# Attention over 4 images: x transposed by VectorE in 32x32 blocks, and the ends of a group regrouped

## The chip, the cores and the metric

The kernel runs on one core of a Trainium2 chip. The metric is the device time of one launch in microseconds; the median of three runs stands for a kernel. A profile of one execution comes with it, taken by the hardware profiler: for each engine (PE is TensorE, PEld its weight loads, DVE is VectorE, ACT is ScalarE, POOL is GpSimd, SP is SyncE, which here only issues transfers) it lists every instruction with start and duration, what it waited for, and every DMA issue. DMA issued from SP and from POOL goes through two queues that share the core's 16 DMA engines.

## The reference

For each of 4 images with 4096 positions and 256 channels, self-attention and a residual:

```python
q = jnp.einsum('bwhc,cd->bwhd', x, Wq) + bq      # 128 wide
k = jnp.einsum('bwhc,cd->bwhd', x, Wk) + bk      # 128 wide
v = jnp.einsum('bwhc,cd->bwhd', x, Wv) + bv      # 256 wide
pq, pk, pv = q.reshape(B, -1, N), k.reshape(B, -1, N), v.reshape(B, -1, N)
energy = jnp.einsum('bcn,bcm->bnm', pq, pk)      # 4096 x 4096 per image
attention = softmax(energy, axis=-1)
out = jnp.einsum('bcm,bnm->bcn', pv, attention).reshape(B, W, H, C)
return gamma * out + x
```

The reshape is a plain one, without a transpose, so a row of pq is not a channel of one position: 32 consecutive positions of q fill one row of 4096. Everything is float32.

## The kernel before, in words

**Numbers in three parts.** To keep float32 accuracy with fast matmuls, every operand is split into three fp32r parts: h (a slightly shrunk copy, made by ScalarE), d and l (two corrections, made by VectorE from h and the original). Each product is then three fast matmuls. `split` (L153), `x_forms`, `qk_forms` and `v_pair_forms` make these parts.

**Steps.** Image b has 8 groups g of 512 query columns (`NG`), and each group 16 steps t (`NU`), each over 256 keys. The loop at L693 runs over all n = 0..511 steps; t is n modulo 16. One step on TensorE is 18 matmuls of 512 columns, in this order: `cross(n+2)` (2, then ScalarE scales them in PSUM), the first half of `attend(n, 0)` (6), `energy(n+2)` (4, then ScalarE takes the exponential into a tile x), pieces of the projection work, and `attend(n, 1)` (6). `upper` makes h of the exponentials on ScalarE, `halves(n+1)` makes l and d on VectorE (L418, L420) and adds the tile into the running softmax sum s (L403): three operations over 128x1024 per step. Buffers l and d have two copies, k three.

**Projections ride along.** While image b is attended, the q, k and v of image b+1 are computed in 16 steps per pair of x units (8 pairs per image). `step(p, engine)` (L555) puts the pieces into TensorE's, ScalarE's and VectorE's order by a count r; for most of the kernel r is t - 1 (modulo 16). At r = 0 (t = 1) TensorE transposes both units of x with a matmul against the identity (`transposed`, L214: 4 transposes of 128x128 per unit) into a PSUM bank; at r = 1..4 ScalarE and VectorE split it; at r = 5 and 6 come the q and k products, at r = 9 to 12 the v products. At r = 12 (t = 13) `load_x` (L200) asks SP to load the next pair of x into the buffer with tag xd. That buffer also holds the d parts of the present pair, so the load waits for the v products at t = 12. Image 0's x is done ahead of the loop, in its own way.

**End of a group.** At t = 15 `emptied(n, 0)` lets ScalarE copy two of the four PSUM accumulators into the tile o (tag o, a single buffer); at t = 0 VectorE empties the other two. Then `finish` (L464) runs as a generator that `proceed` advances once at the end of each step: SP stores both halves of the sum s to DRAM (zd) and reads them back regrouped as y (32 partitions by 4 rows, 8 transfers), so that VectorE can add over partitions: a reduction (L482), a 32x32 block transpose (L488), another reduction, a reciprocal. At t = 3 VectorE adds the two halves of o (L479), at t = 9 it multiplies by the reciprocal (L497), at t = 10 a POOL transfer adds x from DRAM into o (L501), and at t = 13 SP stores o to the output (L504).

**What sets the order.** Each engine's order is the order in which the program names its instructions. SP and POOL issue their transfers in this order too, and each waits at the head of its queue. A new tile with a tag waits until the readers and writers of the buffer's last tile are done, a DMA among them counting as done when it has landed. On SP, step t = 13 names first the x loads (they stand in the "act" part of `step`), later the store of o (`proceed`); the vf stores follow at t = 14 and 0, zd at t = 15, y at t = 0.

Of the kernel before, what the change touches and what calls it, by code (L numbers as in the profile page):

```python
# [9 lines left out]
F32 = mybir.dt.float32  # L10
# [3 lines left out]
ALU = mybir.AluOpType  # L14
AX = mybir.AxisListType
# [5 lines left out]
def kernel(  # L21
# [36 lines left out]
    nc = tc.nc  # L58
# [42 lines left out]
    with ExitStack() as fast:  # L101
# [13 lines left out]

        vall = qkv.tile([P, NU, 2, 3, C], F32R, tag="v", name="v")
        wf = qkv.tile([P, 2, 3, KC, C], F32R, tag="wf", name="wf")
        zd = dram.tile([B * NG, 2, P, NB], F32, tag="zd", name="zd", bufs=1)
        rd = dram.tile([B * NG, NB], F32, tag="rd", name="rd", bufs=1)
        xs4 = work.tile([P, 4, 2, XB], F32, tag="o", name="xs", bufs=1)  # L120
        raw = ppool.tile([P, 2, KC, C], F32, tag="x", name="raw")
# [66 lines left out]
        def bank(name, shape, b, ring):  # L188
            if b:
                tile_ = spare(name, shape)  # L190
                now["turn"] += 1
                return tile_
            pool, tag = next(rings[ring])
            return pool.tile(shape, F32, tag=tag, name=name)
# [5 lines left out]
        def load_x(b, i):  # L200
            if b == B or i >= NI:
                return
            if b == 0:
                t = xs4[:, i % 4]
                if i:
                    nc.sync.dma_start(t, xv[b, i])
                loads["x", b, i] = t
                return
            pair = work.tile([P, 2, 2, XB], F32, tag="xd", name=f"x_{b}_{i}", bufs=1)
            for u in range(2):  # L210
                nc.sync.dma_start(pair[:, u], xv[b, i + u])
                loads["x", b, i + u] = pair[:, u]

        def transposed(b, i):  # L214
            xs = loads.pop(("x", b, i))
            tp = units["xt", b, i] = bank(f"xt_{b}_{i}", [P, KC, 2, P], b, 0)
            for k in range(KC):
                for s in range(2):
                    nc.tensor.transpose(tp[:, k, s, :], xs[:, s, k * P : (k + 1) * P], ident)  # L219

        def x_forms(b, i):

            y = units.pop(("xt", b, i))
            if b == 0:
                if i % 3 < 2:
                    f = ppool.tile([P, 3, KC, 2, P], F32R, tag="ld", name=f"xf_{b}_{i}")
                else:
                    f = work.tile([P, 4, KC, 2, P], F32R, tag="xf", name=f"xf_{b}_{i}", bufs=1)
                f = [f[:, j] for j in range(3)]
            else:  # L230
                if i % 2 == 0:
                    shape = [P, 2, KC, 2, 2, P]
                    f = work.tile(shape, F32R, tag="xf", name=f"xf_{b}_{i}", bufs=1)
                    d = work.tile([P, *shape[2:]], F32R, tag="xd", name=f"xd_{b}_{i}", bufs=1)
                    now["xf"] = [f[:, 0], f[:, 1], d]
                f = [y_[:, :, i % 2] for y_ in now["xf"]]
            units["xf", b, i] = f
            yield from split(*f, y, b == 0 and i > 1)
# [156 lines left out]
        def halves(n):  # L395
            if n >= B * STEPS:
                return
            x, h = units[n]

            def summed():  # L400
                if n % NU:
                    s = now["s"]
                    nc.vector.tensor_tensor(s, s, x, ALU.add)  # L403
                else:
                    now["s"] = x

            def whole():
                s = now["sum"] = now["s"]
                nc.vector.tensor_tensor(s[:, 0, :], s[:, 0, :], s[:, 1, :], ALU.add)

            after = 0 < n < 5
            if not after:
                summed()
            if n == B * STEPS - 1:
                whole()
            ld = ppool.tile([P, 2, 2, NB], F32R, tag="ld", name=f"ld_{n}")
            l, d = ld[:, 0], ld[:, 1]
            nc.vector.tensor_tensor(l, x, h.bitcast(F32), ALU.subtract)  # L418

            nc.vector.scalar_tensor_tensor(  # L420
                d, h.bitcast(F32), 1.0 + E, x, ALU.mult, ALU.subtract
            )
            if n == 2:
                next(vs)
                next(vs, None)
            if after:
                summed()
            units[n] = h, l, d
# [35 lines left out]
        def finish(n, o, s):  # L464
            b, g = divmod(n, NG)
            r4 = rall[:, n, :]
            for i in range(2):
                nc.sync.dma_start(zd[n, i], s[:, i, :])
            yield
            y = q_tile(n, f"y_{n}", F32).rearrange("p j f a -> p (j f) a")  # L470
            for j in range(NJ):
                for i in range(2):
                    nc.sync.dma_start(
                        y[j * 32 : (j + 1) * 32, NJ * i : NJ * (i + 1)],
                        zd[n, i].rearrange("(a p) (j c) -> j p a c", p=32, j=NJ)[j],
                    )
            for _ in range(3):
                yield
            nc.vector.tensor_tensor(o[:, 0], o[:, 0], o[:, 1], ALU.add)  # L479
            for _ in range(3):  # L480
                yield
            nc.vector.tensor_reduce(  # L482
                y[:, 8].rearrange("p (f c) -> p c f", f=NJ),
                y[:, :8].rearrange("p a (c f) -> p c f a", f=NJ),
                AX.X,
                ALU.add,
            )
            nc.vector.transpose(y[:, 9], y[:, 8])  # L488
            nc.vector.tensor_reduce(r4, y[:, 9].rearrange("p (f c) -> p f c", f=NJ), AX.X, ALU.add)
            nc.vector.reciprocal(r4, r4)  # L490
            nc.sync.dma_start(rd[n, :].rearrange("(p j) -> p j", j=NJ), r4)
            yield
            r = o[:, 1, 0]
            nc.sync.dma_start(r, rd[n, :].partition_broadcast(P))
            yield
            yield
            nc.vector.tensor_tensor(  # L497
                o[:, 0], o[:, 0], r.unsqueeze(1).to_broadcast([P, 2, NB]), ALU.mult
            )
            yield  # L500
            nc.gpsimd.dma_start(o[:, 0], xg[b, g], accum_op=ALU.add)  # L501
            for _ in range(3):
                yield
            nc.sync.dma_start(og[b, g], o[:, 0])  # L504
# [50 lines left out]
        def step(n, engine):  # L555

            if n < 0:
                return
            b, u = divmod(n, STEPS)
            i, r = divmod(u, R)  # L560
            b, i = b + 1, 2 * i
            if b >= B:
                return
            made = now["made"]

            def begin(key, pieces):
                made[key] = pieces
                next(pieces)

            if engine == "pe":  # L570
                if r == 0:
                    transposed(b, i)
                    transposed(b, i + 1)
                elif r == 5:
                    products(b, i, 0, (2,))
                    products(b, i + 1, 0, (2,))
                elif r == 6:
                    products(b, i, 0, (0, 1))
                    products(b, i + 1, 0, (0, 1))
                elif r in (9, 11):  # L580
                    products_v(b, i, r // 11, (2,))
                elif r in (10, 12):
                    products_v(b, i, r // 12, (0, 1))
            elif engine == "act":
                if r in (1, 2):
                    begin(("x", r - 1), x_forms(b, i + r - 1))
                elif r in (7, 8):
                    begin(("qk", r - 7), qk_forms(b, i + r - 7))
                elif r in (10, 12):
                    seed_v_pair(b, i, r // 12)  # L590
                    if r == 12:
                        load_x(b + (i + 2) // NI, (i + 2) % NI)
                elif r in (11, 13):
                    begin(("v", r // 13), v_pair_forms(b, i, r // 13))
            else:
                if 1 <= r <= 4:
                    next(made["x", (r - 1) // 2])
                elif r == 5:
                    seed_qk(b, i)
                    seed_qk(b, i + 1)  # L600
                elif 7 <= r <= 10:
                    next(made["qk", (r - 7) // 2])
                    if r % 2 == 0:
                        next(made["qk", (r - 7) // 2], None)
                elif 11 <= r <= 14:
                    next(made["v", (r - 11) // 2])
                    if r % 2 == 0:
                        next(made["v", (r - 11) // 2], None)
# [355 lines left out]
```

## Time and profile before

| | |
|---|---|
| median of 3 runs | 2321.32 us (2320.11 to 2322.51) |
| the profiled execution | 2319.64 us |
| its span, first to last instruction | 2317.9 us |
| TensorE's granted clock | 0.999 |
| DMA | 445.30 MB, mean 192 GB/s |
| SP's queue / POOL's queue, share of 16 DMA engines | 20.6% / 45.5% |

The times in a profile row count from the first instruction of the span. A busy time is the union of the instructions' durations. Matmuls overlap in the pipeline, so the busy share of TensorE alone doesn't say that it was the limit; the chain of waits does: it is followed back from the last instruction, at each step to what released it. In a row of a group, the number after the bar is the busy time in us, then the mean of one in ns, then the idle time ahead of them. DVE operations overlap by some 0.08 us, so the time that one costs on its queue is the distance of two starts. For a transfer the duration is that of issuing it; the landing is told apart.

### The profile page before, as it was taken

To read this page: it belongs to the slowest core of one execution; us is meant where nothing else is said; L and a number is where in the kernel's file an instruction comes from. 1 tells how busy PE (TensorE), PEld (TensorE's weight loads), DVE (VectorE), ACT (ScalarE), POOL (GpSimd) and SP (SyncE) were. 2 spreads that over 40 slices of the span, in tenths; PEclk is the share of its full clock that TensorE was granted. 3 is DMA by queue.
4 is the path that set the end of the run, shared out by engine and by line. 5 is a ranking of instruction groups with operands and counts; after the bars stand their busy time and mean duration, and the time that the engine had idled before them with its cause. 6 is when DMAs were issued, how large, how long until landed. Compare 5 with 4: busy or idle time off the path is not lost.

```text
span 2317.9 us, 31970 instructions
## 1 busy us (share of the span) xinstructions
PE 2307.0 (100%) x10758; PEld 1931.5 (83%) x10758; DVE 2174.3 (94%) x2174; ACT 1796.9 (78%) x2917; POOL 417.1 (18%) x716
## 2 busy tenths in 40 slices
PE   9999999999999999999999999999999999999998
PEld 9888888888888888888888888888888888888887
DVE  8999999999999999999999999999999999888988
ACT  7778777787777777777777777777787777888775
POOL 7111111111221111111122111111112211111110
PEclk9999999999999999999999999999999999999999
DMA  8557765577896776666799667755679855455553
GB/s 273 162 168 207 206 176 154 170 204 205 266 268 184 208 207 179 166 170 194 201 292 267 186 182 207 199 167 165 173 223 289 258 140 141 141 136 149 154 150 97
DMA packets 232190, 445.30 MB, mean 192 GB/s; under 512 B 27986, under 2 KB 109652, under 8 KB 232020
## 3 DMA queue, kind: packets, MB, share of 16 engines
q0 software_dynamic: 101120, 280.54, 45.5%
q1 hardware_dynamic: 130352, 162.38, 20.6%
q8 instruction: 88, 1.44, 0.3%
q14 instruction: 82, 0.67, 0.1%
q10 hardware_dynamic: 548, 0.26, 0.0%
HBM read 321.92 MB, written 120.39 MB: 191 GB/s over the span
## 4 chain that ended last, share of the span: by engine, by line
PE 99%; DVE 0%; ACT 0%; DMA 0%; issue 0%; ACTq 0%; DVEq 0%
PE a L442 40%; PE e L383 20%; PE b L442 20%; PE e L368 10%; PE qv L257 5%; PE v L274 3%; PE xt L219 1%; DMA raw<-in_L_conv_Wk_dram 0%; ACT qv L292 0%; DVE xf L165 0%; PE zp L517 0%; DVE o_last L547 0%; DVE o_last L542 0%; DVE qv L285 0%; DVE o_last L548 0%
## 5 line engine op out<-in xcount | busy, mean ns | idle before, releaser
L386 ACT ACTIVATE x<-e 128x512 f32<-128x512 f32 x960 | 522.4, 596 | 323.6 <-PE e L383 323.5
L369 ACT ACTIVATE e<-e 128x512 f32<-128x512 f32 x1024 | 546.7, 571 | 132.2 <-PE e L368 132.2
L442 PE MATMUL a<-h,v 128*128 128x512 f32 x2048 | 633.5, 390 | 0.0
L442 PE MATMUL a<-ld,v 128*128 128x512 f32 x2048 | 630.9, 389 | 0.0
L442 PE MATMUL b<-ld,v 128*128 128x512 f32 x2048 | 630.8, 389 | 0.0
L418 DVE TENSOR_TENSOR ld<-x,h 128x1024 fp32r<-128x1024 f32 x480 | 584.6, 1218 | 35.1 <-ACT h L392 22.3
L403 DVE TENSOR_TENSOR s<-s,x 128x1024 f32<-128x1024 f32 x480 | 584.2, 1217 | 33.9 <-ACT x L386 32.6
L355 POOL DMA_DIRECT2D k<-kf x512 | 272.5, 532 | 1845.7 <-PE e L383 1745.2
L420 DVE SCALAR_TENSOR_TENSOR ld<-h,x 128x1024 fp32r<-128x1024 f32 x480 | 584.0, 1217 | 0.0
L383 PE MATMUL e<-q,k 128*128 128x512 f32 x2048 | 547.7, 389 | 0.0
L392 ACT ACTIVATE h<-x 128x1024 fp32r<-128x1024 f32 x480 | 510.5, 1064 | 14.3
L442 PEld LDWEIGHTS a<-ld,v 128*128 128x128 f32 x2048 | 384.4, 188 | 80.6
L442 PEld LDWEIGHTS b<-ld,v 128*128 128x128 f32 x2048 | 384.3, 188 | 80.3 <-DVE ld L420 0.2
L383 PEld LDWEIGHTS e<-q,k 128*128 128x128 f32 x2048 | 384.2, 188 | 79.7
L442 PEld LDWEIGHTS a<-h,v 128*128 128x128 f32 x2048 | 379.6, 188 | 74.2
L368 PE MATMUL e<-q,k 128*128 128x512 f32 x1024 | 315.5, 389 | 0.0
L368 PEld LDWEIGHTS e<-q,k 128*128 128x128 f32 x1024 | 191.9, 188 | 39.8
L310 DVE SCALAR_TENSOR_TENSOR f<-f,qv 128x512 fp32r<-128x512 f32 x128 | 85.5, 678 | 0.3
L418 DVE TENSOR_TENSOR ld<-s,h 128x1024 fp32r<-128x1024 f32 x32 | 39.2, 1226 | 46.8 <-ACT h L392 46.8
L257 PE MATMUL qv<-wf,xf 128*128 128x256 f32 x576 | 77.2, 285 | 0.9 <-DVE qv L285 0.4
L257 PEld LDWEIGHTS qv<-wf,xf 128*128 128x128 f32 x576 | 73.7, 191 | 4.1 <-DVE xf L165 0.8
L165 DVE SCALAR_TENSOR_TENSOR vf<-vf,v 128x512 fp32r<-128x512 f32 x96 | 65.2, 679 | 0.0
(88 smaller groups left out, 1126.8 us busy)
## 6 DMA issues: line engine op xcount, KB each, us to landing
k<-kf POOLq DMA_DIRECT2D x512, 384.0 KB, 3.6
vf<-vf SPq DMA_DIRECT2D x96, 384.0 KB, 5.1
v<-vf POOLq DMA_DIRECT2D x96, 384.0 KB, 6.3
kf<-f SPq DMA_DIRECT2D x128, 192.0 KB, 3.7
qd<-f SPq DMA_DIRECT2D x124, 192.0 KB, 3.8
q<-qd POOLq DMA_DIRECT2D x31, 768.0 KB, 6.0
zd<-s SPq DMA_DIRECT2D x62, 256.0 KB, 5.0
y<-zd SPq DMA_DIRECT2D x248, 64.0 KB, 4.4
```

The lines of the kernel that those rows point to most:

```text
L257: nc.tensor.matmul(to[:, s, :], left, right.rearrange("p s a -> p (s a)") if w else right, start=(f == 2 and s == k == 0), stop=(f == 1 an ...
L310: nc.vector.scalar_tensor_tensor(f[:, :, :, j, :], h.bitcast(F32), s, y, ALU.mult, op)
L355: nc.gpsimd.dma_start(t, kf[b, u % NU])
L368: nc.tensor.matmul(e, *forms(n, i, 2), start=True, stop=False, skip_group_check=True)
L369: nc.scalar.mul(e, e, -REST)
L383: nc.tensor.matmul(e, *forms(n, i, f), start=False, stop=(f == 1), skip_group_check=True)
L386: nc.scalar.activation(x[:, i, :], e, AF.Exp, scale=(1.0 + E) ** 3 / E)
L392: nc.scalar.activation(h, units[n], AF.Identity, scale=UPPER)
L403: nc.vector.tensor_tensor(s, s, x, ALU.add)
L418: nc.vector.tensor_tensor(l, x, h.bitcast(F32), ALU.subtract)
L420: nc.vector.scalar_tensor_tensor(d, h.bitcast(F32), 1.0 + E, x, ALU.mult, ALU.subtract)
L442: nc.tensor.matmul(to, vall[:, t, i, f, j * P : (j + 1) * P], units[n][f][:, i, :], start=(t == 0 and i == 0 and f != 1), stop=(t == NU - ...
```

## The change

Three things are changed.

1. For images 1 to 3, `transposed` is no longer 4 TensorE transposes per unit but one VectorE instruction over 128x512, which transposes within blocks of 32x32. To make the result the same, x has to lie differently in SBUF: row j of block q holds what belongs to channels 32q to 32q+31. So a unit is loaded by 8 transfers instead of 1, each of 32 partitions, in contiguous pieces of 32 floats. VectorE transposes at r = 1 and 2; the split's pieces move to r = 3 and 4, on VectorE two in each.
2. The two halves of o are added by a POOL transfer from o to o with accumulation, in place of VectorE's L479.
3. The halves of the sum s are added by VectorE (`whole`, 128x512) at the last step of every group, before the sum is stored; before, only the last group of all did this. So only one half is stored (1 transfer for 2), read back (4 for 8) and reduced (512 columns for 1024).

```diff
-        zd = dram.tile([B * NG, 2, P, NB], F32, tag="zd", name="zd", bufs=1)
+        zd = dram.tile([B * NG, P, NB], F32, tag="zd", name="zd", bufs=1)
...
             for u in range(2):
-                nc.sync.dma_start(pair[:, u], xv[b, i + u])
-                loads["x", b, i + u] = pair[:, u]
+                raw_x = pair[:, u].rearrange("p s f -> p (s f)")
+                for q in range(4):
+                    for k in range(KC):
+                        nc.sync.dma_start(
+                            raw_x[q * 32 : (q + 1) * 32, k * XB : (k + 1) * XB].rearrange(
+                                "j (s c i) -> j s c i", s=2, c=4
+                            ),
+                            xv[b, i + u].rearrange(
+                                "(c j) s (k q i) -> q k j s c i", j=32, k=KC, q=4
+                            )[q, k],
+                        )
+                loads["x", b, i + u] = raw_x
...
             tp = units["xt", b, i] = bank(f"xt_{b}_{i}", [P, KC, 2, P], b, 0)
+            if b:
+                nc.vector.transpose(tp.rearrange("p k s a -> p (k s a)"), xs)
+                return
...
-            if n == B * STEPS - 1:
+            if n % NU == NU - 1:
                 whole()
...
-            for i in range(2):
-                nc.sync.dma_start(zd[n, i], s[:, i, :])
+            nc.sync.dma_start(zd[n], s[:, 0, :])
             yield
             y = q_tile(n, f"y_{n}", F32).rearrange("p j f a -> p (j f) a")
             for j in range(NJ):
-                for i in range(2):
-                    nc.sync.dma_start(
-                        y[j * 32 : (j + 1) * 32, NJ * i : NJ * (i + 1)],
-                        zd[n, i].rearrange("(a p) (j c) -> j p a c", p=32, j=NJ)[j],
-                    )
+                nc.sync.dma_start(
+                    y[j * 32 : (j + 1) * 32, :NJ],
+                    zd[n].rearrange("(a p) (j c) -> j p a c", p=32, j=NJ)[j],
+                )
             for _ in range(3):
                 yield
-            nc.vector.tensor_tensor(o[:, 0], o[:, 0], o[:, 1], ALU.add)
+            nc.gpsimd.dma_start(o[:, 0], o[:, 1], accum_op=ALU.add)
             for _ in range(3):
                 yield
             nc.vector.tensor_reduce(
-                y[:, 8].rearrange("p (f c) -> p c f", f=NJ),
-                y[:, :8].rearrange("p a (c f) -> p c f a", f=NJ),
+                y[:, 4].rearrange("p (f c) -> p c f", f=NJ),
+                y[:, :NJ].rearrange("p a (c f) -> p c f a", f=NJ),
                 AX.X,
                 ALU.add,
             )
...
             if engine == "pe":
-                if r == 0:
-                    transposed(b, i)
-                    transposed(b, i + 1)
-                elif r == 5:
+                if r == 5:
...
             elif engine == "act":
-                if r in (1, 2):
-                    begin(("x", r - 1), x_forms(b, i + r - 1))
+                if r in (3, 4):
+                    begin(("x", r - 3), x_forms(b, i + r - 3))
...
             else:
-                if 1 <= r <= 4:
-                    next(made["x", (r - 1) // 2])
+                if r in (1, 2):
+                    transposed(b, i + r - 1)
+                elif r in (3, 4):
+                    next(made["x", r - 3])
+                    next(made["x", r - 3])
```

More of the change, by code (lines that the diff above doesn't have):

```diff
@@ L487, in finish @@
             )
-            nc.vector.transpose(y[:, 9], y[:, 8])
-            nc.vector.tensor_reduce(r4, y[:, 9].rearrange("p (f c) -> p f c", f=NJ), AX.X, ALU.add)
+            nc.vector.transpose(y[:, 5], y[:, 4])
+            nc.vector.tensor_reduce(r4, y[:, 5].rearrange("p (f c) -> p f c", f=NJ), AX.X, ALU.add)
             nc.vector.reciprocal(r4, r4)
```

## The prediction

> **What bounds the kernel now.** I read the busy times first, then the chain of waits, then one period of 16 steps by windows and by time, and last the DMA queue of SP. In the first fence: the page's busy times and its chain by engine; one period as a window (columns: length, then busy time and count of PE, weight loads, DVE, ACT, POOL, then clock, DMA share, GB/s); and pieces of the chain in order of time (start, length).
>
> ```profile
> PE 2307.0 (100%) x10758; PEld 1931.5 (83%) x10758; DVE 2174.3 (94%) x2174; ACT 1796.9 (78%) x2917; POOL 417.1 (18%) x716
> PE 99%; DVE 0%; ACT 0%; DMA 0%; issue 0%; ACTq 0%; DVEq 0%
> ...
> 815.85:887.66 71.81, 71.81 (x334) 60.00 (x334) 68.69 (x70) 55.77 (x91) 10.15 (x18) 1.00 0.65 183
> ...
> 860.40 0.91 PE e L383 x4
> 861.31 0.87 PE xt L219 x8
> 862.18 0.92 PE a L442 x4
> ...
> 887.66 1.91 PE qv L257 x16
> ```
>
> The chain is TensorE for 99%, and one period shows no gap in it: whatever leaves TensorE's stream is gained, and whatever makes TensorE wait is lost. VectorE has 71.81 - 68.69 = 3.1 us to spare per period. I write t for the step's number modulo 16; in the period shown, t = 0 begins with the `cross` matmuls at 854.34 (quoted below).
>
> **TensorE: the transposes go.** The eight transposes of a pair of x units take 0.87 us of the chain. Images 1 to 3 have 24 pairs (192 transposes in groups of 8), so 24 x 0.87 = 20.9 us are removed. Nothing is put on TensorE instead.
>
> **VectorE.** The rows by shape (count | busy us, mean ns | idle before), and the same engine in order of time, with the matmuls that need its results:
>
> ```profile
> L165 DVE SCALAR_TENSOR_TENSOR xd<-xf,xt 128x512 fp32r<-128x512 f32 x48 | 32.5, 677 | 0.0
> L482 DVE TENSOR_REDUCE y<-y 128x128 f32<-128x1024 f32 x31 | 61.7, 1991 | 0.0
> L488 DVE STREAM_TRANSPOSE y<-y 128x128 f32<-128x128 f32 x31 | 9.7, 312 | 1.1
> L409 DVE TENSOR_TENSOR s<-s 128x512 f32<-128x512 f32 x1 | 0.7, 691 | 0.0
> ...
> 846.45 1.23 DVE L418 TENSOR_TENSOR ld<-x,h 128x1024 fp32r<-128x1024 f32 x1 [0.45 <-PE b L442]
> 850.86 1.23 DVE L418 TENSOR_TENSOR ld<-s,h 128x1024 fp32r<-128x1024 f32 x1 [1.45 <-ACT h L392]
> 870.99 1.22 DVE L479 TENSOR_TENSOR o<-o 128x1024 f32<-128x1024 f32 x1
> 872.13 1.22 DVE L403 TENSOR_TENSOR s<-s,x 128x1024 f32<-128x1024 f32 x1
> 878.40 1.22 DVE L420 SCALAR_TENSOR_TENSOR ld<-h,x 128x1024 fp32r<-128x1024 f32 x1
> 879.54 0.68 DVE L165 SCALAR_TENSOR_TENSOR xf<-xf,xt 128x512 fp32r<-128x512 f32 x1
> 880.14 1.22 DVE L403 TENSOR_TENSOR s<-s,x 128x1024 f32<-128x1024 f32 x1
> 889.76 1.22 DVE L420 SCALAR_TENSOR_TENSOR ld<-h,x 128x1024 fp32r<-128x1024 f32 x1
> ...
> 881.08 0.61 PE L442 MATMUL b<-ld,v 128*128 128x512 f32 x2
> 892.16 0.61 PE L442 MATMUL b<-ld,v 128*128 128x512 f32 x2
> ```
>
> - Added: two 128x512 block transposes, at t = 2 and 3, where the L165 pieces of x stood. No row has this shape. The 128x128 one took 312 ns, so a 512-wide one lies between 0.31 us and four times that, 1.25. I take 0.68, what a 128x512 operation that touches PSUM took, and 0.60 of queue time (879.54 to 880.14): 1.2 us a period.
> - Gone: L479, 872.13 - 870.99 = 1.14 us. L482 reads half as much; between nothing and half of 1.99 us, I take 0.9.
> - Added: `whole` at t = 14, 0.69 us by L409, between two operations one of which sat idle 0.45 us and the next 1.45 us before it. I cost it at nothing; if those idles were gone it would be 0.6 a period.
>
> The sum is 1.2 - 1.14 - 0.9 + 0.6 = -0.2 us of VectorE a period, against 0.87 less TensorE time to hide in. The order matters more: the x pieces, one each at t = 2 to 5, become transposes at t = 2 and 3 and two pieces each at t = 4 and 5. At t = 5 operand d ended at 878.40 + 1.22 = 879.62 and its matmul began at 881.08, 1.46 us of slack; it gains 1.14, loses one piece (0.60) and the 0.87, and keeps 1.13. At t = 7 it is 892.16 - 890.98 = 1.18, plus 1.14 and 0.9, minus two pieces and 0.87: 1.15. So VectorE stays just behind TensorE, and I count no stall. With transposes of 1.25 us the 1.14 more would use all of this up.
>
> ScalarE's two x pieces move to t = 4 and 5, where they come between the `cross` scaling and the exponentials as they did before; nothing. The add of o's halves becomes one POOL transfer of 512 KB at t = 3. What is behind it on POOL is the next k load, which waits for TensorE anyway; what reads its result is L497 six steps later. Nothing, unless POOL's queue is full, which its 10.15 us of 71.81 does not show. The sum's transfers fall from 2 + 8 to 1 + 4 on SP: they are not waited for, nothing either way.
>
> **SP's queue: the part that can undo it.** At t = 13 two x loads become 16, and in SP's order the store of o (L504) stands behind them. The next `emptied` writes o (one buffer) at t = 15, so it waits for that store to land. Rows of this place (a q after the engine: its DMA queue), then the durations of the loads, the landing of the store in the last image, where no x load stands ahead, and of one store beside the v loads:
>
> ```profile
> 840.03 1.20 SPq L211 DMA_DIRECT2D x<-in_x_dram  x2
> 841.33 0.59 SPq L504 DMA_DIRECT2D out_dram<-o  x1
> 854.85 5.08 SPq L473 DMA_DIRECT2D y<-zd  x8
> ...
> 849.36 0.53 POOL L355 DMA_DIRECT2D k<-kf  x1 [4.46 <-PE e L383]
> ...
> 853.70 0.69 ACT L462 ACTIVATE o<-a,gam 128x512 f32<-128x512 f32 x1
> ...
> 854.34 0.62 PE L368 MATMUL e<-q,k 128*128 128x512 f32 x2
> 854.80 0.61 PE L442 MATMUL a<-h,v 128*128 128x512 f32 x2
> ...
> L211 SPq DMA_DIRECT2D x<-in_x_dram x48: 545/583/867, 68.1 to 1702.4; - x48
> ...
> L504 SPq DMA_DIRECT2D out_dram<-o x8: 543/544/545, 1841.1 to 2296.0; - x8
> ...
> DMA to landing us min/median/max: 3.0/3.0/7.2
> ...
> DMA to landing us min/median/max: 9.6/9.6/9.6
> ...
> k<-kf POOLq DMA_DIRECT2D x512, 384.0 KB, 3.6
> rd<-rall SPq DMA_DIRECT2D x31, 2.0 KB, 1.4
> ...
> q1 hardware_dynamic: 130352, 162.38, 20.6%
> ```
>
> The first x load goes out at 840.03, when the buffer xd comes free; call that the gate. ScalarE begins to empty a at gate + 13.67 and ends at 854.39; TensorE needs it at 854.80, 0.41 later. So the store may land up to gate + 14.08 for free, and TensorE waits for what is beyond. Behind `emptied` on ScalarE stand the scaling of e and the next h, on which VectorE's l and d of the next step wait; they are late by the same time, beside and not on top of it. Behind the x loads on SP stand, after the store, the vf and zd stores, some 9 us later than now: their buffers are written again some ten steps on, and the sum is read at t = 6, so nothing.
>
> When is it issued? Each new load moves 32 KB in 256 pieces of 128 B, as many pieces as an old one had of 1 KB (256 KB). Pace per load: at least 0.545 us; at most 1.27, if it went by pieces as in the y loads (5.08/8 = 0.635 for 128 pieces, one wait among them). I take 0.655: the second of the pair's 1.20 us is 0.61, and the gap to the next 0.04. Sixteen make 10.5 us, against 1.30 before. When does it land? 3.0 us after the issue undisturbed, 9.6 at worst. The k load issued at 849.36 (landing after 3.6) flies at the same time; I take 3.8. The store then lands at gate + 14.3, 0.2 us too late.
>
> 22 stores stand behind x loads: 24 pairs issue 23 loads (the last has nothing more to load), and the first of these comes before any store. Twenty at 0.2 make 4 us. Two lie beside the v loads, where the store took 9.6; between 3.8 and that I take 6.5, so gate + 17.0, 2.9 late: 6 us together. **Sum:** -20.9 + 4 + 6 = -11 us. The profiled execution took 2319.64 us (span 2317.9), 1.7 under the median of 2321.32; -11 on the median is **2310 us**. One tenth of a microsecond more per load is 1.6 us of lateness and 22 x 1.6 = 35 us: the forecast stands on an edge.
>
> **The rivals.**
> 1. *The store costs nothing* (pace 0.6 or less, landing 3.5 or less: gate + 13.1): 2321.3 - 20.9 = 2300 us. For it: the shortest load row, 0.545. Against it: that row is a load with none ahead.
> 2. *The wait eats the gain exactly:* stalls of 0.75 to 1.15 us in each period, within 0.2% of before (about what a measurement of this kernel tells from no change): 2317 to 2326.
> 3. *The other side: the store is late for good.* Place: ScalarE's `emptied` at t = 15. It decides from a pace of about 0.72 us per load (16 x 0.72 + 3.8 - 14.08 = 1.24 late, 22 x 1.24 = 27 us against 20.9). At 0.8 it is 2.5 late: 2321 - 21 + 55 + 6 = 2361; at 1.27, 10 late, 2520. For it: the y row's price per piece. Against it: the x rows.
> 4. *The small pieces themselves are slow.* The hardware queue's packets took 0.206 x 16 x 2317.9/130352 = 59 ns each at 1.25 KB. If 128 B cost as much, 16 x 256 of them over 16 engines take 15.0 us, the store lands at about gate + 15.0 + 3.0 = 18, 4 late: 2321 - 21 + 22 x 4 = 2388. Against it: rd's 2 KB, 128 pieces of 16 B, landed after 1.4 us. The Trainium skill, in "DMA: Bandwidth & Descriptors", section Specifications, speaks for this rival: it puts the smallest transfer for full rate at 512 B and says that a smaller one is read, changed and written. By that rule the time would be this rival's; the 1.4 us row shows no such price, though for a single small transfer.
> 5. *VectorE becomes the bound* (transposes over 1.25 us): another 0.5 us a pair is 24 x 0.5 = 12 us, so 2322 with my stalls. Against it: the 312 ns row.
>
> **How the numbers follow.** My forecast's case (stalls of 0 to 0.5 us, 2302 to 2317) 0.33; rival 1 0.12; rival 2 0.14; rival 3 0.29; rival 4 0.07; rival 5 0.05, mostly slower. Faster 0.45, same 0.14, slower 0.41. The range takes in all but the tails of rivals 3 and 4: 2299 to 2385; the likeliest case alone is 2302 to 2317.
>
> **What would show it.** After: no xt rows on TensorE beyond the 64 of image 0; a period near 70.94 us plus the stall; SP with 16 x rows of about 0.6 us, the store issued 10.5 us behind the first; ScalarE's L462 waiting for the DMA out_dram<-o, and TensorE idle before a at t = 0. The 128x512 transposes near 0.68 us. Pace over 0.7 or a store landing after more than 4.3 us makes me wrong upwards; a store landing within 3.5 us makes me wrong downwards; waits of TensorE for DVE ld (L420) would show that I mis-sized VectorE.

## The result, and the profile after

The changed kernel takes **2337.84 us** (median of 6 runs, 2332.99 to 2339.47) against 2321.27 before: a ratio of 1.0068, 95% interval 1.0056 to 1.0081. It is slower by 0.7%, inside the range and on the wrong side of the forecast.

The page of the changed kernel: busy times, and the chain by engine. Then its list of waits (in total us, times, longest us):

```profile
PE 2301.2 (99%) x10566; PEld 1916.1 (82%) x10566; DVE 2162.4 (93%) x2222; ACT 1798.1 (77%) x2917; POOL 446.5 (19%) x747
PE 84%; SPq 9%; DMA 5%; ACT 1%; issue 1%; DVE 0%; ACTq 0%; DVEq 0%
...
L228 DVE STREAM_TRANSPOSE xt<-x x48: 711/718/723, 82.6 to 1750.3; 128x512 f32<-128x512 f32 x48
```

```profile
ACT o L475 <- DMA out_dram<-o: 32.2, 22, 5.8
PE a L455 <- ACT o L475: 23.1, 20, 5.4
```

Before, the chain was 99% TensorE. Now SP's queue holds 9% of it, transfers 5%. VectorE got no busier. The waits name the place: ScalarE's emptying of the accumulators (L475 here, L462 before) waits 22 times for the store of o, and TensorE 20 times for ScalarE.

POOL loads the v of the next image around the end of an image (here 583 to 702 us and 1163 to 1282); a period with neither these loads beside it nor a stretch of halved clock is called quiet. One quiet period, and the worst one, as windows from one t = 0 to the next (columns as in the prediction); below them, the four stretches in which the granted clock was 0.5:

```profile
932.77:1004.36 71.59, 71.23 (x325) 59.11 (x325) 68.34 (x73) 55.78 (x91) 11.09 (x19) 1.00 0.67 184
566.90:643.54 76.64, 71.24 (x324) 59.12 (x324) 68.33 (x73) 55.78 (x91) 19.62 (x35) 0.98 0.89 258
...
641.20:648.00 6.80, 4.46 (x11) 3.49 (x12) 4.50 (x5) 3.81 (x6) 0.00 (x0) 0.50 0.93 351
1221.50:1228.30 6.80, 4.54 (x11) 3.61 (x12) 4.58 (x5) 3.80 (x6) 0.00 (x0) 0.50 1.03 390
1300.00:1303.40 3.40, 3.40 (x10) 2.62 (x9) 2.72 (x3) 2.52 (x5) 0.11 (x1) 0.50 1.04 411
1375.10:1378.50 3.40, 3.40 (x9) 2.67 (x8) 2.72 (x3) 2.41 (x5) 0.00 (x0) 0.51 0.69 260
```

Through the end of that quiet period, in two fences: the chain (start, length), then the timeline's rows of SP, ScalarE and TensorE:

```profile
998.88 0.61 SPq L214
...
999.59 3.92 DMA out_dram<-o
...
1003.62 0.70 ACT o L475
...
1004.36 1.20 PE a L455 x4
```

```profile
989.07 10.42 SPq L214 DMA_DIRECT2D x<-in_x_dram  x16
999.59 0.59 SPq L515 DMA_DIRECT2D out_dram<-o  x1
...
1003.62 0.69 ACT L475 ACTIVATE o<-a,gam 128x512 f32<-128x512 f32 x1 [0.75 <-DMA out_dram<-o]
...
1004.36 0.73 PE L455 MATMUL a<-h,v 128*128 128x512 f32 x2 [0.35 <-ACT o L475]
1004.93 0.62 PE L455 MATMUL a<-ld,v 128*128 128x512 f32 x2
```

The queue answers the prediction's rows one by one. Sixteen loads take 10.42 us, 0.65 each with the gaps between them; the store goes out at 999.59, 10.52 us behind the gate at 989.07, and lands 3.92 later. ScalarE starts at 1003.62, after 0.75 us without work, and TensorE's row shows 0.35 us of waiting.

That row counts from the end of the matmuls before it, and in a stream without a stall a matmul starts before the end of the last one. Counted by starts the wait is longer: in the kernel with the store ahead (the first experiment below) `a` begins 988.88 - 974.11 = 14.77 us behind the gate, here 1004.36 - 989.07 = 15.29, so 0.52 us late. A period without the wait takes 70.92 us there; this one lost 0.67.

The 24 periods with projections took 1740.6 us, from 65.22 to 1805.82, and 1702.8 in the kernel with the store ahead, from 66.19 to 1769.00 (the first of them takes 71.65 us in both, with no store to wait for). The 37.8 us of loss are TensorE's 23.1 us of waiting by the rows, 7.9 us at clock 0.5 (half of the 15.8 us for which the four stretches show TensorE busy), and 6.8 us that are left. That is 0.31 us for each of 22 stalls, about what the quiet period lost beyond its row (0.67 - 0.35).

### The profile page after: what moved, and what is told of

Read it like the earlier page. It is cut to its first block, busy times and chain, and to the rows that moved or that the text cites. A ratio compares the mean times of both kernels' runs of the same rounds, so it can differ in the third digit from the quotient of the medians.

```text
span 2336.0 us, 31907 instructions
## 1 busy us (share of the span) xinstructions
PE 2301.2 (99%) x10566; PEld 1916.1 (82%) x10566; DVE 2162.4 (93%) x2222; ACT 1798.1 (77%) x2917; POOL 446.5 (19%) x747
## 3 DMA queue, kind: packets, MB, share of 16 engines
q1 hardware_dynamic: 199424, 146.14, 20.1%
## 4 chain that ended last, share of the span: by engine, by line
PE 84%; SPq 9%; DMA 5%; ACT 1%; issue 1%; DVE 0%; ACTq 0%; DVEq 0%
PE a L455 34%; PE e L396 17%; PE b L455 17%; SPq L214 9%; PE e L381 8%; PE qv L270 5%; DMA out_dram<-o 4%; PE v L287 2%; DMA x<-in_x_dram 1%; ACT o L475 1%; PE xt L232 0%; DMA xs<-in_x_dram 0%; ACT qv L305 0%; DVE ld L433 0%; ACTq L475 0%
## 5 line engine op out<-in xcount | busy, mean ns | idle before, releaser
L455 PE MATMUL a<-h,v 128*128 128x512 f32 x2048 | 635.4, 391 | 23.4 <-ACT o L475 23.1
L433 DVE SCALAR_TENSOR_TENSOR ld<-h,x 128x1024 fp32r<-128x1024 f32 x480 | 584.1, 1217 | 0.0
L165 DVE SCALAR_TENSOR_TENSOR vf<-vf,v 128x512 fp32r<-128x512 f32 x96 | 65.2, 680 | 0.1
```

The lines of the kernel that those rows point to most:

```text
L433: nc.vector.scalar_tensor_tensor(d, h.bitcast(F32), 1.0 + E, x, ALU.mult, ALU.subtract)
L455: nc.tensor.matmul(to, vall[:, t, i, f, j * P : (j + 1) * P], units[n][f][:, i, :], start=(t == 0 and i == 0 and f != 1), stop=(t == NU - ...
```

## The experiments

### The store of o ahead of the x loads

```diff
             nc.gpsimd.dma_start(o[:, 0], xg[b, g], accum_op=ALU.add)
-            for _ in range(3):
+            for _ in range(2):
                 yield
             nc.sync.dma_start(og[b, g], o[:, 0])
```

> The changed kernel with one thing moved: the store of o is named one step earlier (t = 12), so on SP it stands ahead of the x loads and not behind them. Theory 1 (the store behind 16 loads is the whole loss): the 24 periods fall from 1740.6 us in all to 24 x 70.9 = 1702, so 2338 - 38 = 2300 us (2298 to 2304); ScalarE's waits for out_dram<-o vanish, and the granted clock is 1.000 over the 24 periods. Rival 2 (VectorE is the bound, or the 128-byte pieces slow the k and v loads): the periods stay above 71.5 us and the time above 2315 us.

Measured: **2299.96 us**, ratio to before 0.9912 (0.9895 to 0.9928). SP and ScalarE at the end of a quiet period of this kernel, and that period as a window:

```profile
972.31 0.60 SPq L515 DMA_DIRECT2D out_dram<-o  x1
974.11 10.45 SPq L214 DMA_DIRECT2D x<-in_x_dram  x16
...
987.78 0.69 ACT L475 ACTIVATE o<-a,gam 128x512 f32<-128x512 f32 x1
...
917.96:988.88 70.92, 70.92 (x325) 59.22 (x324) 68.34 (x73) 55.66 (x91) 11.05 (x19) 1.00 0.68 186
```

The same 16 loads take the same 10.45 us, but nothing that ScalarE needs stands behind them. It empties the accumulators without an idle time, the period is 70.92 us without a gap on TensorE, and the whole loss is gone, with the forecast gain of 21 us in its place. This is a version faster than both kernels, by one step's difference in when a store is named. It refutes at once that VectorE or the small pieces as such cost the time: both are unchanged here.

### The loads alone, and the ends alone

Two runs take the change apart from the side of the kernel before. In the first, x is loaded in 16 transfers of 256 pieces of 128 bytes, to the same places as before, and TensorE still transposes:

```diff
-                nc.sync.dma_start(pair[:, u], xv[b, i + u])
+                for c in range(8):
+                    at = slice(c * 32, (c + 1) * 32)
+                    nc.sync.dma_start(pair[:, u, :, at], xv[b, i + u][:, :, at])
```

> The kernel before, TensorE's transposes kept, with x of images 1 to 3 loaded to the same places by 16 transfers a pair in place of 2, each of 128 partitions in 256 pieces of 128 bytes. Theory 1: SP needs 0.655 us for each, the store of o goes out 10.5 us behind the first, and the stalls come without the gain: 2321 + 38 = 2359 us (2345 to 2375). Rival 2 (VectorE's transposes and not the loads are the loss): 2321 to 2325 us.

Measured: **2358.26 us**, ratio 1.0157 (1.0140 to 1.0174). Its SP and ScalarE at the end of a quiet period, and two periods as windows, a quiet one and the first one:

```profile
1076.62 10.37 SPq L213 DMA_DIRECT2D x<-in_x_dram  x16
1087.10 0.59 SPq L506 DMA_DIRECT2D out_dram<-o  x1
...
1091.09 0.69 ACT L464 ACTIVATE o<-a,gam 128x512 f32<-128x512 f32 x1 [0.68 <-DMA out_dram<-o]
...
1019.41:1091.83 72.42, 72.14 (x333) 59.93 (x333) 68.61 (x71) 55.91 (x91) 10.12 (x18) 1.00 0.66 181
67.05:146.44 79.39, 75.33 (x333) 61.88 (x332) 67.08 (x69) 55.03 (x90) 8.97 (x17) 0.96 0.53 142
```

The loads by themselves bring the wait of the changed kernel (0.68 us on ScalarE here), without any transpose on VectorE. The total met the expectation partly by luck: 7.6 us of the 37 lie in the first period (79.39 against 71.81, with a mean clock of 0.96), where TensorE's transposes waited for a first pair that now lands later, which I had not counted; the other periods lost 30, not 38.

In the second run, parts 2 and 3 are made alone (o's halves added by POOL, the sum's halves added every group), with x as before.

```diff
-            if n == B * STEPS - 1:
+            if n % NU == NU - 1:
                 whole()
...
-            nc.vector.tensor_tensor(o[:, 0], o[:, 0], o[:, 1], ALU.add)
+            nc.gpsimd.dma_start(o[:, 0], o[:, 1], accum_op=ALU.add)
```

> The kernel before with parts 2 and 3 of the change alone (o's halves added by a POOL transfer, halves of the sum added every group), x loaded and transposed as before. Theory 1: TensorE's stream is untouched and VectorE only gets freer, so 2321 us within 3 us. The rival by which the group's end costs the time: 2335 us or more.

Measured: 2320.64 us, ratio 1.0002 (0.9993 to 1.0012). No difference: VectorE's time was not on the path before, and neither POOL's transfer nor the additions at t = 14 hold anything up.

### How many loads ahead of the store

If order on SP is the cause, time must follow the number of loads ahead of the store. One run puts the last 4 of the 16 behind it: they are kept in a list, which is issued and emptied at the end of the step, after `proceed` has named the store (`load_rest`).

```diff
-                        nc.sync.dma_start(
+                        pair_ = (
...
+                        if u == 1 and q >= 2:
+                            late_loads.append(pair_)
+                        else:
+                            nc.sync.dma_start(*pair_)
...
             proceed()
+            load_rest()
```

> The changed kernel with the last 4 of the 16 loads of a pair behind the store of o and not ahead of it, so the store goes out 2.6 us sooner, 7.9 us behind the first load. Theory 1: the 0.65 us of the quiet periods vanish (2.6 is more than their lateness), of the two stalls beside the v loads (5.4 and 4.7 us) 2 to 3 us each stay, and the clock holds: 2300 to 2310 us. Rival (what counts is that the loads share the DMA engines, not the order on SP): 2330 us or more.

The other run adds 4 transfers of the same shape, DRAM to DRAM, which nothing uses:

```diff
+            for m in range(4):
+                waste = dram.tile([32, XB], F32, tag=f"waste{m}", name=f"waste{m}_{b}_{i}", bufs=1)
+                nc.sync.dma_start(
+                    waste.rearrange("j (s c i) -> j s c i", s=2, c=4),
+                    xv[b, i].rearrange("(c j) s (k q i) -> q k j s c i", j=32, k=KC, q=4)[m, 0],
+                )
```

> The changed kernel with 4 more transfers of the x loads' shape (DRAM to DRAM, their result unused) behind the 16, so ahead of the store of o. At 0.655 us each the store goes out 2.6 us later in each of 22 periods. If lateness is paid one for one and no more: 2338 + 22 x 2.6 = 2395 us. If the clock's halving after a stall (3.41 or 6.83 us at 0.5 in four of the changed kernel's periods) comes with every stall of about 3 us: 22 x 1.7 to 3.4 more, 2433 to 2470 us.

Measured: **2308.33 us** with 12 ahead (ratio 0.9950, 0.9933 to 0.9966) and **2454.72 us** with 20 ahead (1.0583, 1.0565 to 1.0600). A period of each without v loads beside it, SP's rows and the window, first with 12:

```profile
976.11 7.84 SPq L232 DMA_DIRECT2D x<-in_x_dram  x12
984.05 0.59 SPq L526 DMA_DIRECT2D out_dram<-o  x1
984.68 2.72 SPq L204 DMA_DIRECT2D x<-in_x_dram  x4
...
919.96:990.88 70.92, 70.92 (x326) 59.18 (x325) 68.32 (x73) 55.66 (x91) 11.05 (x19) 1.00 0.68 185
```

And with 20, with TensorE's wait for ScalarE in the whole trace:

```profile
970.44 10.46 SPq L214 DMA_DIRECT2D x<-in_x_dram  x16
980.95 2.58 SPq L225 DMA_DIRECT2D waste<-in_x_dram  x4
983.62 0.58 SPq L521 DMA_DIRECT2D out_dram<-o  x1
...
912.81:989.87 77.06, 72.56 (x325) 60.10 (x325) 68.74 (x73) 55.89 (x91) 11.06 (x19) 0.97 0.63 177
...
PE a L461 <- ACT o L481: 98.9, 22, 5.7
```

With 12 ahead the store goes out 7.94 us behind the first load and the quiet periods are whole again, with the same 16 loads sharing the same DMA engines; what is left of the loss (8 us over 2299.96, 6 in the profiled execution) is in the periods beside and just after the v loads. With 20, TensorE waits 98.9 us in all, 75.8 more than in the changed kernel, where 22 x 2.6 = 57 was the bare lateness: the store also took longer to land (5.4 us in this period, 3.92 in the quiet one of the changed kernel). The time rose by 117. Most of the remainder goes with the clock, whose mean was 0.97 in this period and 1.00 in the other: the trace has 22 stretches at clock 0.5, in which TensorE was busy for 92 us, and half of that is 46, against 7.9 in the changed kernel. Both runs fall into the bands expected of the theory with the order and with the clock.

### What parts 2 and 3 are for

Part 1 was run alone, behind and ahead of the store, and then with each of the other parts undone, all three with the store ahead. Part 1 alone is the changed kernel with the lines of parts 2 and 3 put back (cut here to those that carry it):

```diff
-            if n % NU == NU - 1:
+            if n == B * STEPS - 1:
                 whole()
...
-            nc.sync.dma_start(zd[n], s[:, 0, :])
+            for i in range(2):
+                nc.sync.dma_start(zd[n, i], s[:, i, :])
...
-            nc.gpsimd.dma_start(o[:, 0], o[:, 1], accum_op=ALU.add)
+            nc.vector.tensor_tensor(o[:, 0], o[:, 0], o[:, 1], ALU.add)
...
-                y[:, :NJ].rearrange("p a (c f) -> p c f a", f=NJ),
+                y[:, :8].rearrange("p a (c f) -> p c f a", f=NJ),
```

> The kernel before with part 1 of the change alone (x by 16 loads, transposes on VectorE); the halves of o added by VectorE and the sum regrouped in full, as before. Theory 1: the stalls of the changed kernel stay, 2338 us, plus what VectorE lacks: its slack of 1.1 us at t = 5 falls to about 0, so 0 to 0.5 us in each of 24 periods: 2338 to 2350 us. A rival by which the group's end costs the time (POOL's transfer from o to o, the additions at t = 14): back to 2300 to 2321 us.

Measured: 2356.21 us, ratio 1.0152 (1.0135 to 1.0169), 18 over the changed kernel and 6 over the upper end of what I expected. The same kernel with the store's `range(3)` made `range(2)`:

> Part 1 of the change alone, with the store of o ahead of the x loads. In the run of part 1 alone one pair had no store behind its loads, and its period was 72.06 us: that is what VectorE leaves without parts 2 and 3. Theory (VectorE is the bound without parts 2 and 3): 24 x (72.06 - 71.81) = +6 us over before, 2327 us (2322 to 2331), and TensorE's weight loads wait for DVE ld. Rival (the 18 us that part 1 alone cost over the changed kernel were more stalls behind the store): 2300 us.

Measured: 2318.04 us, ratio 0.9990 (0.9980 to 0.9999): 18 over the kernel with all three parts in the same order, 4 below the expected band. Its waits of TensorE, three pieces of the chain at t = 7, and a quiet period:

```profile
PEld b L455 <- DVE ld L433: 20.8, 27, 0.8
PE b L455 <- DVE ld L433: 9.3, 23, 0.4
...
958.29 1.91 PE qv L270 x16
...
962.16 1.23 DVE ld L433
...
963.43 0.73 PE b L455 x2
...
926.32:998.01 71.69, 71.29 (x325) 59.04 (x324) 69.54 (x73) 55.65 (x91) 10.15 (x18) 1.00 0.66 185
```

Here VectorE is the bound: 71.69 - 70.92 = 0.77 us a period, 24 x 0.77 = 18 us. The place is t = 7: behind the 16 `qv` matmuls (products for q and k), TensorE's next `b` matmuls wait for L433, which makes d.

With the store ahead, part 2 undone:

```diff
-            nc.gpsimd.dma_start(o[:, 0], o[:, 1], accum_op=ALU.add)
+            nc.vector.tensor_tensor(o[:, 0], o[:, 0], o[:, 1], ALU.add)
```

> The changed kernel with the store of o ahead, and part 2 undone: o's halves added by VectorE again (1.14 us at t = 3). By the prediction's slack (1.13 us left at t = 5, 1.15 at t = 7) this uses it up and no more: 2300 to 2307 us. If the slack was taken 0.5 us too high: 2300 + 24 x 0.5 = 2312 us.

Measured: 2299.91 us, ratio 0.9914 (0.9897 to 0.9931). And with part 3 undone, both halves stored, read back and reduced:

```diff
-            if n % NU == NU - 1:
+            if n == B * STEPS - 1:
                 whole()
...
-            nc.sync.dma_start(zd[n], s[:, 0, :])
+            for i in range(2):
+                nc.sync.dma_start(zd[n, i], s[:, i, :])
...
-                y[:, :NJ].rearrange("p a (c f) -> p c f a", f=NJ),
+                y[:, :8].rearrange("p a (c f) -> p c f a", f=NJ),
```

> The changed kernel with the store of o ahead, and part 3 undone: both halves of the sum stored, read back and reduced (0.9 us more at t = 6, 0.6 less at t = 14); o's halves still added by POOL. Parts 2 and 3 both undone cost 18 us (2318.04 against 2299.96), part 2 alone undone nothing (2299.91). If either part suffices: 2300 us (2299 to 2303). If part 3 is the one that is needed, because its saving comes at t = 6, where VectorE was latest: 2318 us (2310 to 2320).

Measured: 2300.79 us, ratio 0.9914 (0.9898 to 0.9931). So either part is enough to give VectorE the time for the transposes; only without both is it late.

## Why the prediction was wrong, by its own steps

**TensorE's gain: right.** 24 x 0.87 = 20.9 us; the kernel with the store ahead is 2320.8 - 2300.0 = 20.8 under before, and its period 71.81 - 70.92 = 0.89 shorter.

**VectorE: right, and closer than it needed to be.** A transpose took 0.718 us (0.68 taken), the period's busy time is 68.34 us (68.69 - 0.2 forecast). The slack of 1.15 us at t = 7 agrees with the runs: without parts 2 and 3 it would be 1.15 - 1.14 - 0.9 = -0.89, and 0.77 us were lost there; without one of them it stays at or above zero, and nothing was lost. For part 1 alone I had reckoned with t = 5 and not with t = 7, which is why its expectation was 12 us over the changed kernel at most, and it came out at 18.

**The place of the loss: right.** It is the one that the forecast and rival 3 share: the store of o behind 16 loads, and ScalarE's `emptied` at t = 15 waiting for it. In the quiet periods the pace (0.655 taken, 0.65 measured), the issue at gate + 10.5 and the landing (3.8 taken, 3.92 measured) held. The pace of 0.72 from which rival 3 was to decide was not reached there; beside the v loads it was passed.

**The step that failed is the sum over the 22 stores.** "Twenty at 0.2 make 4 us" and "two lie beside the v loads ... 2.9 late: 6 us together" came to 10 us; 37.8 were lost. Three terms were too small or missing:

1. A quiet period lost 0.67 us and not 0.2. The store landed at gate + 10.52 + 3.92 = 14.44, 0.36 past the deadline of gate + 14.08. But the deadline was set 0.16 too late: it left nothing for the time from the landing to ScalarE's start (0.11) and from ScalarE's end to TensorE's start (0.05). So `a` began 0.52 late. The other 0.15 were lost after the stall, 0.11 of it between the first two pairs of matmuls, which start 0.57 apart there (1004.36 to 1004.93) and 0.46 in a stream without a stall. That the 0.36 agrees with the 0.35 of the wait's row is luck: the two count from different points. The sixteen quiet periods behind a late store lost 0.43 to 1.02 us each, 11.5 in all.
2. Beside the v loads I kept the pace of the quiet periods. SP's rows in the worst one, a piece of the chain there, and those waits of SP's x loads in the whole trace that an earlier transfer ended:

```profile
623.22 13.57 SPq L214 DMA_DIRECT2D x<-in_x_dram  x16
636.88 0.59 SPq L515 DMA_DIRECT2D out_dram<-o  x1
...
642.80 0.69 ACT L475 ACTIVATE o<-a,gam 128x512 f32<-128x512 f32 x1 [5.80 <-DMA out_dram<-o]
...
623.22 8.37 DMA x<-in_x_dram
...
SPq L214 <- DMA x<-in_x_dram: 4.0, 4, 1.6
SPq L214 <- DMA qd<-f: 3.4, 4, 1.0
...
SPq L214 <- DMA kf<-f: 2.1, 3, 0.8
```

   The loads took 13.57 us there, 0.85 each. The landing (under 6 us from 636.88) was within the 6.5 I took; the pace made it 5.4 us late, not 2.9. The issues themselves did not get slower. SP's transfers use eight semaphores in turn, and a load waits for the landing of the transfer that used its semaphore last, eight places earlier: the ninth of these loads goes out at 631.61, when the first, issued at 623.22, has landed after 8.37 us. In the quiet period the loads landed within 4.3 us, less than eight issues of 0.65 take, and none waited so; all eleven waits of this kind lie beside the v loads. And six periods were long, not two: two beside the v loads, the one after each of these, and two more. They lost 26 us, with the waits, the clock and the restarts.
3. The clock was not in the sum at all. It costs half of the 15.8 us in which TensorE worked at 0.5, 7.9 us. Without it the time would have been about 2330 us, still above the 2326 up to which rival 2 counts as the same: the first two terms alone put it on the slower side.

On the clock, the Trainium skill in "TensorE: Matmul & The Clock Gate", section "Part 1: The HAM clock gate", says that TensorE falls to half its clock after an idle window of about 3.4 us, in windows that run on freely. This trace agrees in the half (0.50) and in the lengths (two stretches of 3.4, two of 6.8), and in the windows: the four stretches shown begin 580.3, 78.5 and 75.1 us apart, which is 170, 23 and 22 times 3.413. It differs in the idle time: about 2 us within one window was enough. Waits of 2.0 and 2.4 us were followed by a slow stretch here, one of 2.3 us with 12 loads ahead and one of 3.1 us with part 1 alone were not. What tells them apart is how a wait lies to these windows: those of 2.0 and 2.4 us fell whole into one, those of 2.3 and 3.1 us into two, as 0.99 and 1.30, and 1.48 and 1.59. In the 24 periods of every trace of this case, each full-speed window with 1.98 us or more of idle time in TensorE's rows was followed by a slow stretch, and none with 1.94 or less was; so whether a stall of 2 or 3 us halves the clock goes by where it falls. These idle times are by rows whose ends are modelled.

Of the other rivals, 4 (small pieces slow in themselves) would have kept its cost in the kernel with the store ahead, which has the same pieces and none of the loss. The page of the changed kernel says the same: SP's queue moved half as many packets again, in no larger a share of the DMA engines' time (20.1% against 20.6%).

```profile
q1 hardware_dynamic: 199424, 146.14, 20.1%
```

The 512-byte rule of the Trainium skill that I had cited beside this rival ("DMA: Bandwidth & Descriptors", section Specifications) does not show in these loads: their pieces of 128 bytes landed in a median of 2.8 us. Rival 1 was never reached in the changed kernel: no store landed by gate + 14.08 behind 16 loads (the earliest at about gate + 14.17). Rival 5 fell with the transposes' 0.718 us.

**Why the side was wrong.** I saw that 0.1 us per load is worth 35 us, took pace and landing for 20 of the 22 stores from quiet rows, and put the point estimate where nearly all of them are kind at once. The lateness can't be negative: any spread around a deadline adds to the mean, and a stall brings costs of its own.

What stays open: in two periods after the v loads (from 1299 and 1374 on) the store went out at the usual 10.5 us but landed about 2.0 and 0.9 us later than in the quiet ones. With 16 loads in the kernel before this didn't come in the same periods; with part 1 alone it came in the first of them (5.95 us from 1381.74). What held those transfers up is not shown.

## What to carry to other kernels

When a load is split into more transfers, price the queue and not the load: find what stands behind it on the same queue, who waits for that, and by when; 16 transfers at 0.65 us are 10 us for whatever comes next. A transfer whose landing frees a single buffer should be named ahead of loads that nobody needs soon; here that one move was worth 38 us. Near a deadline, sum over the late cases and not over the median one, follow the landing through to the engine that needs it (0.16 us here), and add to each stall what restarting costs.

## What the runs showed that I had not expected

- The time of issuing a load hardly depends on the size of its pieces: 256 pieces of 128 bytes took 0.61 us each in a row, and so did 256 of 1 KB (the second of a pair). Pieces of 128 bytes had no cost of their own that these runs show.
- Beside the v loads the same 16 issues took 13.57 us and not 10.42: SP waited between them for the landing of its transfer eight places earlier, 9.5 us in 11 waits over the whole trace.
- A 32x32 block transpose of 128x512 from SBUF to PSUM takes 0.718 us, where L165, an elementwise operation of the same shape, takes 0.68.
- A stall of TensorE costs more than its row shows: 0.3 us in the short ones, and 1.7 to 2.3 us more where the clock is halved in or after it.
